# First stage reordered, normalization of later tiles on GpSimd, transposes set singly between matmuls

## The chip, the cores and the metric

The kernel runs on one core of a Trainium2 chip. The metric is the device time of one execution in microseconds, the median of several runs. The engines are TensorE (PE in the profile, with its weight loads as PEld), VectorE (DVE), ScalarE (ACT), GpSimd (POOL), and SyncE (SP), which here only issues DMAs.

## The reference

```python
xn = _layernorm(x, axis=-1)                       # x: 4 x 512 x 512, fp32
q = einsum('bpd,hde->bphe', xn, W_Q) + b_Q        # 16 heads of 128; k and v likewise
scores = where(causal, q k^T / sqrt(128), -100000)
s = einsum('bqhe,hed->bqd', softmax(scores) v, W_O) + b_O
g = silu(ffn(xn))                                 # gate, up (1408), silu, down, each with scales
out = x + s * g
```

## The kernel before

**Precision.** Every fp32 operand of a matmul is held as two fp32r parts: `hi`, a rounded copy made by ScalarE, and `lo`, the rest, made by a subtraction on VectorE or GpSimd. A product takes three matmuls. `mm3` (line 90) issues them for one chunk of the contraction: hi with lo, hi with hi, lo with hi. A projection has four chunks, so 12 matmuls.

**Order of the work.** All of it is written out by hand under a manual schedule: each engine runs its instructions in the order in which the program emits them, and waits in place for what an instruction needs. There are four batches of 512 tokens, each in four tiles `t` of 128, and 16 heads in groups of two. The attention loop (line 525) takes 64 steps `n`: group by group, within a group batch by batch, within a batch the two heads.

**One step of the loop.** `softmax` (272) issues the scores of head `n` (three banks), the row minima and sums (VectorE, ScalarE) and the scaling by GpSimd (line 316). `fill` then issues half of the work that the step has on the side: for the first head of a pair `project_v` (232) of two tiles. `turn_p` (319) transposes the probabilities through DRAM. Then come q and k of head `n+1` (`project`, 241), the product with v of head `n-1` (`attend`, 376), and the other half of `fill`.

**Normalization.** `ln_stats` (182, VectorE) and `ln_sd` (190, ScalarE) give mean and deviation of a tile; `ln_normalize` (208, VectorE: a reciprocal and one tensor_scalar) gives `xn`. `ln_transpose` (217) transposes a tile in four steps on TensorE into one PSUM bank, from pool `ps_st` for even tiles and `ps_mm` for odd ones; ScalarE copies the hi part, and `ln_low` (227, VectorE) makes the lo part. For batch `b+1` this happens in the first head of batch `b`, in group 0 only, so at n = 0, 2 and 4: the four `ln_normalize` stand between q and k (593), the four transposes and low parts after the rest of `fill` (606). Then the x tiles of batch `b+2` are loaded (610).

**PSUM.** Eight banks: three in `ps_st` (scores, transposes of even tiles), five in `ps_mm` (projections, v, products, transposes of odd tiles). A bank is taken again only when its last reader is done.

**First stage** (lines 461 to 514). SP loads the four x tiles of batch 0, then Wq, Wk of head 0 and Wv (two pieces). `warm_up` (202) keeps TensorE busy with 24 transposes meanwhile. Loaded weights wait in `pending`; `split_pending` (150) emits their hi copies (ScalarE) and lo parts (GpSimd). The first q and k are projected in two halves of 256 tokens (`parts=2`), both halves in one bank. `project` is a generator: a `next` issues one half's matmuls, and the following `next` its evacuation. The order is tiles 0 and 1, first half of q, tiles 2 and 3, first half of k, second halves of q and k, then `project_v` of tile 0.

Of the kernel before, what the change touches and what calls it, by code (L numbers as in the profile page):

```python
# [10 lines left out]
F32 = mybir.dt.float32  # L11
# [7 lines left out]
P = 128  # L19
# [1 line left out]
IGNORE = -100000.0  # L21
EPS = 1e-5
BIG = 3.0e38
WARM = 24
LOW_BITS = (1 << 12) - 1


# [15 lines left out]
def kernel(  # L43
# [46 lines left out]
    def mm3(ps, a, b, first, last):  # L90
        nc.tensor.matmul(ps, a.hi, b.lo, start=first, stop=False)  # L91
        nc.tensor.matmul(ps, a.hi, b.hi, start=False, stop=False)  # L92
        nc.tensor.matmul(ps, a.lo, b.hi, start=False, stop=last)  # L93


    with ExitStack() as at:
        lnp = at.enter_context(tc.tile_pool(name="lnp", bufs=NT))
# [14 lines left out]
        def load_x(b, t):  # L112
            xt = lnp.tile([P, D], F32, name="xt", tag="xt")
            nc.sync.dma_start(out=xt, in_=x[b, ts(t, P), :])
            x_in[b, t] = xt
# [14 lines left out]
            load_on[0].dma_start(out=r, in_=src)  # L130
            return r

        def split_w(dst, raw):
            nc.scalar.copy(dst.hi, raw)
            nc.gpsimd.tensor_tensor(dst.lo, raw, dst.hi32, ALU.subtract)

        def flat(s):
            return Split(s.hi.rearrange("p c e -> p (c e)"), s.lo.rearrange("p c e -> p (c e)"))
# [8 lines left out]

        pending = []

        def split_pending(n):  # L150

            for due, dst, raw in [p for p in pending if p[0] <= n]:
                split_w(dst, raw)
            pending[:] = [p for p in pending if p[0] > n]

        def prepare(due, dst, src, name):
# [3 lines left out]
        def prepare_qk(h, due, due_k=None):  # L160
            for d, src, n, when in ((wq, w_q, "wq", due), (wk, w_k, "wk", due_k or due)):
                d[h] = weight(wqkp, [P, ND, E], f"{n}{h}", n)
                prepare(when, flat(d[h]), src[h].rearrange("p c e -> p (c e)"), f"{n}r{h}")

        def prepare_v(g, due):
            wv[g] = weight(wvop, [P, ND, HG * E], f"wv{g}", "wv")
            half = ND // 2
            for i in range(2):
                c = slice(i * half, (i + 1) * half)
                src = w_v[g][:, c, :].rearrange("p c e -> p (c e)")  # L170
                prepare(due, flat(wv[g][:, c, :]), src, f"wvr{g}_{i}")
# [10 lines left out]
        def ln_stats(b, tt):  # L182

            mv = small.tile([P, len(tt), 2], F32, name="mv")
            for k, t in enumerate(tt):
                st = small.tile([P, 6], F32, name="st")
                nc.vector.bn_stats(out=st, in_=x_in[b, t])
                nc.vector.bn_aggr(out=mv[:, k, :], in_=st)
            mv_of[b, tuple(tt)] = mv

        def ln_sd(b, tt):
            mv = mv_of.pop((b, tuple(tt)))
            sd = small.tile([P, len(tt)], F32, name="sd")
            nc.scalar.activation(sd, mv[:, :, 1], AF.Sqrt, bias=eps)
            for k, t in enumerate(tt):
                ln_of[b, t] = mv[:, k, :], sd[:, k : k + 1]

        def table(func):

            nc.scalar.activation(small.tile([P, 1], F32, name="junk"), eps, func)  # L200
# [4 lines left out]
            for k in range(WARM):  # L205
                nc.tensor.transpose(junk[:, k % NT, :], ident, ident)

        def ln_normalize(b, t):
            xt = x_in.pop((b, t))
            mv, sd = ln_of.pop((b, t))  # L210
            rstd = small.tile([P, 1], F32, name="rstd")
            nc.vector.reciprocal(rstd, sd)
            xn = lnp.tile([P, D], F32, name="xn")
            nc.vector.tensor_scalar(xn, xt, mv[:, 0:1], rstd, ALU.subtract, ALU.mult)
            xn_of[b, t] = xn

        def ln_transpose(b, t):
            xn = xn_of.pop((b, t))
            pool, tag = ((ps_st, "st"), (ps_mm, "mm"))[t % 2]
            tr = pool.tile([P, ND, P], F32, name="tr", tag=tag)  # L220
            for c in range(ND):
                nc.tensor.transpose(tr[:, c, :], xn[:, ts(c, P)], ident)
            to = xnT[b][:, :, ts(t, P)]
            nc.scalar.copy(to.hi, tr)
            lo_of[b, t] = lambda: nc.vector.tensor_tensor(to.lo, tr, to.hi32, ALU.subtract)  # L225

        def ln_low(b, t):
            lo_of.pop((b, t))()
# [2 lines left out]

        def project_v(g, b, t):
            ps = ps_mm.tile([P, HG * E], F32, name="psv", tag="mm")
            for c in range(ND):
                mm3(ps, xnT[b][:, c, ts(t, P)], wv[g][:, c, :], c == 0, c == ND - 1)
            v = weight(vp, [P, HG * E], f"v{g}_{b}_{t}", "v")
            nc.scalar.copy(v.hi, ps)
            nc.vector.tensor_tensor(v.lo, ps, v.hi32, ALU.subtract)
            v_of.setdefault((g, b), []).append(v)

        def project(b, h, w, bias, name, parts=1):

            ps = ps_mm.tile([P, S], F32, name="ps" + name, tag="mm")
            both = qkp.tile([P, 2, S], F32R, name=name, tag=name)
            q = Split(both[:, 0, :], both[:, 1, :])
            q.both = both
            for k in range(parts):
                at_ = ts(k, S // parts)
                for c in range(ND):
                    mm3(ps[:, at_], w[:, c, :], xnT[b][:, c, at_], c == 0, c == ND - 1)  # L250
                yield
                nc.scalar.activation(  # L252
                    q.hi[:, at_], ps[:, at_], AF.Identity, bias=bias[:, h : h + 1]
                )
                nc.vector.scalar_tensor_tensor(  # L255
                    q.lo[:, at_], ps[:, at_], bias[:, h : h + 1], q.hi32[:, at_],
                    ALU.add, ALU.subtract,
                )
            yield q

# [199 lines left out]

        with tc.manual_schedule():
            nc.gpsimd.memset(eps, EPS)
            for t in range(NT):
                load_x(0, t)
            prepare_qk(0, -4, -3)
            prepare_v(0, -2)
            bq_sb, bk_sb, bv_sb, gs_sb, us_sb = small_const()
            table(AF.Sqrt)
# [4 lines left out]
            nc.gpsimd.memset(ones, 1.0)  # L473
            nc.gpsimd.memset(mask, 0.0)
            make_causal_mask(nc, mask[:, S - P :], mask_val=IGNORE / SCALE)
            ln_stats(0, [0])
            ln_sd(0, [0])
            ln_stats(0, [1])
            ln_sd(0, [1])
            ln_normalize(0, 0)  # L480
            split_pending(-4)
            ln_transpose(0, 0)
            ln_stats(0, [2])
            ln_sd(0, [2])
            ln_normalize(0, 1)
            ln_low(0, 0)
            split_pending(-3)
            ln_transpose(0, 1)
            ln_low(0, 1)
            q_of = project(0, 0, wq[0], bq_sb, "q", 2)  # L490
            k_of = project(0, 0, wk[0], bk_sb, "k", 2)
            next(q_of)
            split_pending(-2)
            prepare_qk(1, -1)
            ln_stats(0, [3])
            ln_sd(0, [3])
            ln_normalize(0, 2)
            ln_transpose(0, 2)
            ln_normalize(0, 3)
            ln_low(0, 2)  # L500
            ln_transpose(0, 3)
            next(k_of)
            ln_low(0, 3)
            next(q_of)
            next(k_of)
            split_pending(-1)
            table(AF.Exp)
            qT = next(q_of)
            kT = next(k_of)
            for t in range(NT):  # L510
                load_x(1, t)
            bo_bc = load_const(b_o.broadcast_to([P, D]), [P, D], "bo_bc")
            ds_bc = load_const(down_s.broadcast_to([P, D]), [P, D], "ds_bc")
            project_v(0, 0, 0)

            load_on[0] = nc.scalar
            heads = [(g, b, i) for g in range(NG) for b in range(B) for i in range(HG)]
# [7 lines left out]
            for n, (g, b, i) in enumerate(heads):  # L525
# [12 lines left out]
                def fill(ks):  # L538
                    for t in ks:
                        if i == 0 and not (n == 0 and t == 0):  # L540
                            project_v(g, b, t)
                        if i == HG - 1 and prev is not None:
                            project_out(*prev, t, zs[prev])
# [40 lines left out]
                if nxt is not None:  # L584
                    if ln_b is not None and n != 1:
                        ln_stats(ln_b, range(NT))
                    nh = nxt[0] * HG + nxt[2]
                    *_, qT = project(nxt[1], nh, wq[nh], bq_sb, "q")
                    if n == 0:
                        ln_sd(ln_b, range(NT))  # L590
                        table(AF.Exp)
                    if ln_next:
                        for t in range(NT):
                            ln_normalize(b + 1, t)
                if nxt is not None:
                    *_, kT = project(nxt[1], nh, wk[nh], bk_sb, "k")
                    raw = raw_next
# [4 lines left out]
                if ln_b is not None and n > 0:  # L602
                    ln_sd(ln_b, range(NT))
                    table(AF.Exp)
                if ln_next:
                    fill(range(half, NT))
                    for t in range(NT):
                        ln_transpose(b + 1, t)
                        ln_low(b + 1, t)
                    if b + 2 < B:  # L610
                        for t in range(NT):
                            load_x(b + 2, t)
# [191 lines left out]
```

## Time and profile before

| | us |
|---|---|
| median of 3 runs | 1222.99 (1222.97 to 1223.63) |
| profiled execution, time | 1222.41 |
| profiled execution, span of the trace | 1220.6 |
| PE / PEld busy | 1206.5 / 1052.7 |
| DVE / ACT / POOL busy | 827.1 / 525.3 / 301.7 |
| first scores of head 0 start | 20.58 |
| first attention step's end (scores of head 1 start) | 34.20 |
| feed-forward part starts | 974.0 |

A row of the timeline has the start and the duration in us, the engine, the line in the code, the instruction with its output and inputs, how many rows were merged (x4), and in brackets the idle time before it with what ended it. A row of the waits names the waiting instruction, what it waited for, the sum in us, the number of times and the longest. A row of the clock by stretches gives for each stretch the busy time and count of each engine, the clock that TensorE was granted (1.00 is full), the share of DMA and its rate.

### The profile page before, as it was taken

How to read it: one execution, taken by the hardware profiler on the slowest of the kernel's cores; microseconds unless marked ns; L12 is line 12 of the kernel's file. 1: busy time of each engine (PE TensorE's matmuls, PEld its weight loads, DVE VectorE, ACT ScalarE, POOL GpSimd, SP SyncE). 2: the span in 40 equal slices, each digit the busy share in tenths (PEclk: the TensorE clock that was granted, in tenths of full speed). 3: DMA queues.
4: the chain of work that ended last, by engine and by line, in shares of the span. 5: the costliest groups of instructions: out<-in, count | busy, mean ns of one | idle time of the engine just before them, and what ended most of it. 6: DMA issues, size and time to landing. Idle time of an engine off the chain costs nothing.

```text
span 1220.6 us, 18887 instructions
## 1 busy us (share of the span) xinstructions
PE 1206.5 (99%) x6514; PEld 1052.7 (86%) x6514; DVE 827.1 (68%) x2044; ACT 525.3 (43%) x1169; POOL 301.7 (25%) x433
## 2 busy tenths in 40 slices
PE   8999999999999999999999999999999999999997
PEld 8888888888888888888888888888888888888886
DVE  6897777777777777777877676767677533434343
ACT  5654444444445445444544454445444342323231
POOL 4212321232123213321412141214121341212010
PEclk9999999999999999999999999999999999999999
DMA  4454456656665667566655565555544893627241
GB/s 161 138 175 147 145 165 206 206 179 190 190 207 174 203 198 218 181 208 192 211 182 173 178 189 175 177 185 173 173 156 156 272 317 93 207 87 213 80 147 38
DMA packets 117912, 215.55 MB, mean 177 GB/s; under 512 B 13232, under 2 KB 45744, under 8 KB 117808
## 3 DMA queue, kind: packets, MB, share of 16 engines
q1 hardware_dynamic: 74016, 134.51, 34.4%
q10 hardware_dynamic: 29376, 53.26, 14.2%
q0 software_dynamic: 14416, 26.48, 7.9%
q8 instruction: 53, 0.87, 0.3%
q14 instruction: 51, 0.42, 0.1%
HBM read 135.17 MB, written 79.04 MB: 175 GB/s over the span
## 4 chain that ended last, share of the span: by engine, by line
PE 95%; DVE 3%; ACT 1%; DMA 0%; issue 0%; SPq 0%; DVEq 0%; ACTq 0%
PE z L387 10%; PE pd L667 7%; PE pg L667 7%; PE pu L667 7%; PE pso L91 5%; PE psv L91 5%; PE pso L92 5%; PE pso L93 5%; PE psv L93 5%; PE psv L92 5%; PE psq L91 5%; PE psq L92 5%; PE psq L93 5%; PE psk L91 5%; PE psk L92 5%; PE psk L93 5%
## 5 line engine op out<-in xcount | busy, mean ns | idle before, releaser
L316 POOL TENSOR_SCALAR p<-p,rtot 128x512 f32<-128x512 f32 (+3 forms) x256 | 148.2, 598 | 675.1 <-DVE rtot L315 675.1
L312 ACT ACTIVATE p<-p,nmax 128x512 f32<-128x512 f32 (+3 forms) x256 | 140.9, 552 | 147.3 <-DVE nmax L298 147.3
L358 DVE TENSOR_TENSOR ptl<-ptr,pth 128x640 fp32r<-128x640 f32 x126 | 133.7, 1099 | 1.4 <-ACT pth L357 1.4
L330 DVE STREAM_TRANSPOSE sq<-p 128x256 f32<-128x256 f32 x378 | 113.3, 361 | 0.0
L298 DVE CUSTOM_DVE_ANT_0 p<-sc,mask 128x512 f32<-128x512 f32 (+2 forms) x192 | 96.5, 552 | 0.3 <-PE sc L93 0.3
L252 ACT ACTIVATE k<-psk,consts 128x512 fp32r<-128x512 f32 (+1 forms) x65 | 44.2, 681 | 108.7 <-PE psk L93 108.6
L252 ACT ACTIVATE q<-psq,consts 128x512 fp32r<-128x512 f32 (+1 forms) x65 | 44.3, 682 | 97.2 <-PE psq L93 72.6
L357 ACT CAST pth<-ptr 128x640 fp32r<-128x640 f32 x126 | 84.9, 724 | 0.1
L413 DVE TENSOR_TENSOR a<-pso,a 128x512 f32<-128x512 f32 x108 | 72.1, 686 | 17.7 <-PE pso L93 16.4
L255 DVE SCALAR_TENSOR_TENSOR k<-psk,consts,k 128x512 fp32r<-128x512 f32 (+1 forms) x65 | 48.0, 739 | 52.8 <-ACT k L252 52.7
L693 DVE SCALAR_TENSOR_TENSOR hd<-pu,consts,sg 128x512 f32<-128x512 f32 x44 | 33.0, 751 | 66.8 <-PE pu L667 62.2
L315 DVE RECIPROCAL rtot<-tot 128x1 f32<-128x1 f32 x256 | 41.6, 162 | 42.7 <-ACT p L312 36.3
L91 PE MATMUL sc<-k,q 128*128 128x512 f32 (+2 forms) x192 | 65.7, 342 | 1.7 <-DVE xl L225 1.7
L93 PE MATMUL sc<-k,q 128*128 128x512 f32 (+2 forms) x192 | 64.7, 337 | 0.0
L92 PE MATMUL sc<-k,q 128*128 128x512 f32 (+2 forms) x192 | 64.7, 337 | 0.0
L255 DVE SCALAR_TENSOR_TENSOR q<-psq,consts,q 128x512 fp32r<-128x512 f32 (+1 forms) x65 | 47.6, 732 | 7.6 <-ACT q L252 7.6
L312 ACT ACTIVATION_READ_ACCUMULATOR p<-p,nmax 128x1 f32 x256 | 47.8, 187 | 0.0
L91 PEld LDWEIGHTS sc<-k,q 128*128 128x128 f32 x192 | 36.2, 188 | 7.9 <-DVE xl L225 3.5
L723 ACT ACTIVATE o<-o 128x512 f32<-128x512 f32 (+1 forms) x17 | 10.3, 607 | 68.8 <-DVE o L722 68.8
L92 PEld LDWEIGHTS sc<-k,q 128*128 128x128 f32 x192 | 36.2, 189 | 3.6
L93 PEld LDWEIGHTS sc<-k,q 128*128 128x128 f32 x192 | 36.1, 188 | 2.6
L691 ACT ACTIVATE sg<-pg,consts 128x512 f32<-128x512 f32 x44 | 30.3, 688 | 17.0 <-PE pg L667 17.0
(734 smaller groups left out, 3811.6 us busy)
## 6 DMA issues: line engine op xcount, KB each, us to landing
turn<-sq SPq DMA_DIRECT2D x63, 640.0 KB, 3.8
ptr<-turn SPq DMA_DIRECT2D x252, 160.0 KB, 3.4
acc<-a SPq DMA_DIRECT2D x124, 256.0 KB, 3.7
a<-acc ACTq DMA_DIRECT2D x108, 256.0 KB, 2.8
xt<-in_x SPq DMA_DIRECT2D x16, 256.0 KB, 4.1
wor<-in_w_o ACTq DMA_DIRECT2D x16, 256.0 KB, 4.5
fa<-acc SPq DMA_DIRECT2D x16, 256.0 KB, 5.9
fx<-in_x SPq DMA_DIRECT2D x16, 256.0 KB, 6.9
```

The source lines that it names most:

```text
L91: nc.tensor.matmul(ps, a.hi, b.lo, start=first, stop=False)
L92: nc.tensor.matmul(ps, a.hi, b.hi, start=False, stop=False)
L93: nc.tensor.matmul(ps, a.lo, b.hi, start=False, stop=last)
L252: nc.scalar.activation(q.hi[:, at_], ps[:, at_], AF.Identity, bias=bias[:, h : h + 1])
L255: nc.vector.scalar_tensor_tensor(q.lo[:, at_], ps[:, at_], bias[:, h : h + 1], q.hi32[:, at_], ALU.add, ALU.subtract,)
L298: nc.vector.tensor_tensor_reduce(out=of[t], in0=where[t], in1=add, scale=-SCALE, scalar=BIG, op0=ALU.add, op1=ALU.min, accum_out=nmax[t],)
L312: nc.scalar.activation(of[t], of[t], AF.Exp, bias=nmax[t], scale=-1.0, accum_out=tot)
L316: nc.gpsimd.tensor_scalar(of[t], of[t], rtot, 1.0, ALU.mult, ALU.mult)
L330: nc.vector.transpose(dst.rearrange("p a s i -> p s a i"), src.rearrange("p (s a i) -> p s a i", s=n, i=Q),)
L358: nc.vector.tensor_tensor(dst(pt.lo), src, dst(pt.hi32), ALU.subtract)
L387: nc.tensor.matmul(o, v, p_, start=k == 0, stop=k == len(todo) - 1)
L667: nc.tensor.matmul(ps, l, r, start=first and k == 0, stop=last and k == len(pairs) - 1)
```

## The change

The loads, splits, normalizations and projections of the first stage change their order. The tiles 2 and 3 of batch 0, and all tiles of the later batches, are normalized on GpSimd; the reciprocals stay on VectorE. The low parts of Wv of group 0 are made on VectorE. `warm_up` has 20 transposes. `mm3_all` takes the place of `mm3` in the projections of q, k and v: first hi with hi for all four chunks, then the products with the first operand's lo part, then those with the second's; in `project` the second operand is x. After each of its matmuls it takes one entry from `side`, if there is any. At n = 0, 2 and 4 `side` holds, for each tile of the next batch, its four transposes and then its low part (20 entries), so that they stand one by one between the 24 matmuls of `project_v` for tiles 2 and 3. The halves of q and k get a tile of `ps_mm` each. In the first stage v of tile 0 moves ahead of the second halves, the table load for Exp ahead of the casts of Wv, and the split of head 1's weights behind the last evacuation.

```diff
@@ -21,7 +21,7 @@
 IGNORE = -100000.0
 EPS = 1e-5
 BIG = 3.0e38
-WARM = 24
+WARM = 20
 LOW_BITS = (1 << 12) - 1
 
 
@@ -92,6 +92,21 @@
         nc.tensor.matmul(ps, a.hi, b.hi, start=False, stop=False)
         nc.tensor.matmul(ps, a.lo, b.hi, start=False, stop=last)
 
+    def mm3_all(ps, pairs):
+        todo = [
+            (getattr(a, i), getattr(b, k))
+            for i, k in (("hi", "hi"), ("lo", "hi"), ("hi", "lo"))
+            for a, b in pairs
+        ]
+        for n, (l, r) in enumerate(todo):
+            nc.tensor.matmul(ps, l, r, start=n == 0, stop=n == len(todo) - 1)
+            if side:
+                side.pop(0)()
+    side = []
 
     with ExitStack() as at:
         lnp = at.enter_context(tc.tile_pool(name="lnp", bufs=NT))
@@ -130,9 +145,9 @@
             load_on[0].dma_start(out=r, in_=src)
             return r
 
-        def split_w(dst, raw):
+        def split_w(dst, raw, on=nc.gpsimd):
             nc.scalar.copy(dst.hi, raw)
-            nc.gpsimd.tensor_tensor(dst.lo, raw, dst.hi32, ALU.subtract)
+            on.tensor_tensor(dst.lo, raw, dst.hi32, ALU.subtract)
 
         def flat(s):
             return Split(s.hi.rearrange("p c e -> p (c e)"), s.lo.rearrange("p c e -> p (c e)"))
@@ -147,10 +162,10 @@
 
         pending = []
 
-        def split_pending(n):
+        def split_pending(n, on=nc.gpsimd):
 
             for due, dst, raw in [p for p in pending if p[0] <= n]:
-                split_w(dst, raw)
+                split_w(dst, raw, on)
             pending[:] = [p for p in pending if p[0] > n]
 
         def prepare(due, dst, src, name):
@@ -205,24 +220,37 @@
             for k in range(WARM):
                 nc.tensor.transpose(junk[:, k % NT, :], ident, ident)
 
-        def ln_normalize(b, t):
+        def ln_normalize(b, t, on=nc.vector):
             xt = x_in.pop((b, t))
             mv, sd = ln_of.pop((b, t))
             rstd = small.tile([P, 1], F32, name="rstd")
             nc.vector.reciprocal(rstd, sd)
             xn = lnp.tile([P, D], F32, name="xn")
-            nc.vector.tensor_scalar(xn, xt, mv[:, 0:1], rstd, ALU.subtract, ALU.mult)
+            on.tensor_scalar(xn, xt, mv[:, 0:1], rstd, ALU.subtract, ALU.mult)
             xn_of[b, t] = xn
 
         def ln_transpose(b, t):
+            for step in ln_transposes(b, t):
+                step()
+        def ln_transposes(b, t):
             xn = xn_of.pop((b, t))
             pool, tag = ((ps_st, "st"), (ps_mm, "mm"))[t % 2]
-            tr = pool.tile([P, ND, P], F32, name="tr", tag=tag)
-            for c in range(ND):
-                nc.tensor.transpose(tr[:, c, :], xn[:, ts(c, P)], ident)
             to = xnT[b][:, :, ts(t, P)]
-            nc.scalar.copy(to.hi, tr)
-            lo_of[b, t] = lambda: nc.vector.tensor_tensor(to.lo, tr, to.hi32, ALU.subtract)
+            tr = []
+            def step(c):
+                if c == 0:
+                    tr.append(pool.tile([P, ND, P], F32, name="tr", tag=tag))
+                nc.tensor.transpose(tr[0][:, c, :], xn[:, ts(c, P)], ident)
+                if c == ND - 1:
+                    nc.scalar.copy(to.hi, tr[0])
+                    lo_of[b, t] = lambda: nc.vector.tensor_tensor(
+                        to.lo, tr[0], to.hi32, ALU.subtract
+                    )
+            return [lambda c=c: step(c) for c in range(ND)]
 
         def ln_low(b, t):
             lo_of.pop((b, t))()
@@ -231,8 +259,7 @@
 
         def project_v(g, b, t):
             ps = ps_mm.tile([P, HG * E], F32, name="psv", tag="mm")
-            for c in range(ND):
-                mm3(ps, xnT[b][:, c, ts(t, P)], wv[g][:, c, :], c == 0, c == ND - 1)
+            mm3_all(ps, [(xnT[b][:, c, ts(t, P)], wv[g][:, c, :]) for c in range(ND)])
             v = weight(vp, [P, HG * E], f"v{g}_{b}_{t}", "v")
             nc.scalar.copy(v.hi, ps)
             nc.vector.tensor_tensor(v.lo, ps, v.hi32, ALU.subtract)
@@ -240,21 +267,17 @@
 
         def project(b, h, w, bias, name, parts=1):
 
-            ps = ps_mm.tile([P, S], F32, name="ps" + name, tag="mm")
             both = qkp.tile([P, 2, S], F32R, name=name, tag=name)
             q = Split(both[:, 0, :], both[:, 1, :])
             q.both = both
             for k in range(parts):
                 at_ = ts(k, S // parts)
-                for c in range(ND):
-                    mm3(ps[:, at_], w[:, c, :], xnT[b][:, c, at_], c == 0, c == ND - 1)
+                ps = ps_mm.tile([P, S // parts], F32, name="ps" + name, tag="mm")
+                mm3_all(ps, [(w[:, c, :], xnT[b][:, c, at_]) for c in range(ND)])
                 yield
-                nc.scalar.activation(
-                    q.hi[:, at_], ps[:, at_], AF.Identity, bias=bias[:, h : h + 1]
-                )
+                nc.scalar.activation(q.hi[:, at_], ps, AF.Identity, bias=bias[:, h : h + 1])
                 nc.vector.scalar_tensor_tensor(
-                    q.lo[:, at_], ps[:, at_], bias[:, h : h + 1], q.hi32[:, at_],
-                    ALU.add, ALU.subtract,
+                    q.lo[:, at_], ps, bias[:, h : h + 1], q.hi32[:, at_], ALU.add, ALU.subtract
                 )
             yield q
 
@@ -460,9 +483,11 @@
 
         with tc.manual_schedule():
             nc.gpsimd.memset(eps, EPS)
-            for t in range(NT):
-                load_x(0, t)
+            load_x(0, 0)
+            load_x(0, 1)
             prepare_qk(0, -4, -3)
+            load_x(0, 2)
+            load_x(0, 3)
             prepare_v(0, -2)
             bq_sb, bk_sb, bv_sb, gs_sb, us_sb = small_const()
             table(AF.Sqrt)
@@ -473,45 +498,44 @@
             nc.gpsimd.memset(ones, 1.0)
             nc.gpsimd.memset(mask, 0.0)
             make_causal_mask(nc, mask[:, S - P :], mask_val=IGNORE / SCALE)
-            ln_stats(0, [0])
-            ln_sd(0, [0])
-            ln_stats(0, [1])
-            ln_sd(0, [1])
+            for t in range(2):
+                ln_stats(0, [t])
+                ln_sd(0, [t])
             ln_normalize(0, 0)
+            ln_normalize(0, 1)
+            ln_stats(0, [2])
             split_pending(-4)
             ln_transpose(0, 0)
-            ln_stats(0, [2])
+            ln_transpose(0, 1)
+            ln_low(0, 0)
+            ln_low(0, 1)
             ln_sd(0, [2])
-            ln_normalize(0, 1)
-            ln_low(0, 0)
             split_pending(-3)
-            ln_transpose(0, 1)
-            ln_low(0, 1)
+            ln_stats(0, [3])
+            ln_sd(0, [3])
+            table(AF.Exp)
+            ln_normalize(0, 2, nc.gpsimd)
+            ln_normalize(0, 3, nc.gpsimd)
+            split_pending(-2, nc.vector)
+            prepare_qk(1, -1)
             q_of = project(0, 0, wq[0], bq_sb, "q", 2)
             k_of = project(0, 0, wk[0], bk_sb, "k", 2)
             next(q_of)
-            split_pending(-2)
-            prepare_qk(1, -1)
-            ln_stats(0, [3])
-            ln_sd(0, [3])
-            ln_normalize(0, 2)
+            next(k_of)
             ln_transpose(0, 2)
-            ln_normalize(0, 3)
+            ln_transpose(0, 3)
             ln_low(0, 2)
-            ln_transpose(0, 3)
-            next(k_of)
             ln_low(0, 3)
+            project_v(0, 0, 0)
             next(q_of)
             next(k_of)
-            split_pending(-1)
-            table(AF.Exp)
             qT = next(q_of)
             kT = next(k_of)
+            split_pending(-1)
             for t in range(NT):
                 load_x(1, t)
             bo_bc = load_const(b_o.broadcast_to([P, D]), [P, D], "bo_bc")
             ds_bc = load_const(down_s.broadcast_to([P, D]), [P, D], "ds_bc")
-            project_v(0, 0, 0)
 
             load_on[0] = nc.scalar
             heads = [(g, b, i) for g in range(NG) for b in range(B) for i in range(HG)]
@@ -591,7 +615,7 @@
                         table(AF.Exp)
                     if ln_next:
                         for t in range(NT):
-                            ln_normalize(b + 1, t)
+                            ln_normalize(b + 1, t, nc.gpsimd)
                 if nxt is not None:
                     *_, kT = project(nxt[1], nh, wk[nh], bk_sb, "k")
                     raw = raw_next
@@ -603,10 +627,12 @@
                     ln_sd(ln_b, range(NT))
                     table(AF.Exp)
                 if ln_next:
+                    for t in range(NT):
+                        side.extend(ln_transposes(b + 1, t))
+                        side.append(lambda t=t: ln_low(b + 1, t))
                     fill(range(half, NT))
-                    for t in range(NT):
-                        ln_transpose(b + 1, t)
-                        ln_low(b + 1, t)
+                    while side:
+                        side.pop(0)()
                     if b + 2 < B:
                         for t in range(NT):
                             load_x(b + 2, t)
```

## The prediction

> **What bounds it now.** I read the page first: busy times, then the waits of TensorE, then the timeline of the first 100 us engine by engine, then the clock by stretches.
>
> ```profile
> PE 1206.5 (99%) x6514; PEld 1052.7 (86%) x6514; DVE 827.1 (68%) x2044; ACT 525.3 (43%) x1169; POOL 301.7 (25%) x433
> ```
>
> TensorE is busy for all but 14 us of 1220.6, and the chain that ended last is 95% TensorE. So only its idle time and its clock can be won, and the waits tell where they lie:
>
> ```profile
> PE psq L91 <- DVE xl L225: 2.1, 1, 2.1
> PE sc L91 <- DVE xl L225: 1.7, 4, 0.6
> ...
> PE tr L222 <- DVE k L255: 0.7, 1, 0.7
> PE psq L91 <- DVE q L255: 0.4, 1, 0.4
> ```
>
> The first and last row belong to the first stage (before 20.58 us), the others to the changes of batch. I number these T1, T2, T3 (heads 0, 2, 4). In the clock by stretches (the column before the last two is the granted clock), the first wait costs more than itself:
>
> ```profile
> 8.00:10.00 2.00, 0.10 (x1) 0.00 (x0) 1.19 (x2) 2.00 (x6) 2.00 (x2) 1.00 0.08 28
> 10.00:12.00 2.00, 1.75 (x9) 1.76 (x10) 1.90 (x6) 0.80 (x2) 2.00 (x3) 0.64 0.64 176
> 12.00:14.00 2.00, 2.00 (x12) 2.00 (x11) 1.31 (x1) 0.18 (x1) 1.03 (x1) 0.51 0.92 330
> ```
>
> TensorE idles from 8.1 to 10.25 us, and then has half its clock from 10.56 to 13.99: 256-column matmuls start 0.21 us apart there, 0.12 later.
>
> **Two rules of the Trainium skill.** "TensorE: Matmul & The Clock Gate", Part 1, says that the clock is halved after an idle window of 3413 ns, and that the windows run freely. The rows above agree: 3.43 us at half clock after a window with 2.15 us of idle. A window need not be wholly idle, then. At T2 about 1.25 us of idle (62.25, 64.17 and 65.36 us below) fell into 3.4 us and the clock stayed at 1.00. I put the threshold between 1.25 and 2.15 us per window, from this trace. "GPSIMD Engine Reference", 1. Specifications, says that GpSimd shares its SBUF interfaces with VectorE, which meets VectorE instructions in a two-port mode or with two SBUF inputs. The trace agrees: VectorE's normalization takes 0.55 us alone and 1.31 beside GpSimd's subtraction (10.34 to 13.04 us).
>
> ```profile
> 12.01 1.31 DVE L214 TENSOR_SCALAR xn<-xt,mv,rstd 128x512 f32<-128x512 f32 x1
> ...
> 58.85 0.14 DVE L212 RECIPROCAL rstd<-sd 128x1 f32<-128x1 f32 x1
> 59.02 0.55 DVE L214 TENSOR_SCALAR xn<-xt,mv,rstd 128x512 f32<-128x512 f32 x1
> ```
>
> **First stage, loads.** SP issues one load per 0.45 us. Wq moves from place 5 to 3, Wk from 6 to 4, x tiles 2, 3 from 3, 4 to 5, 6. By place the loads landed at 3.6, under 4.4, about 4.8, 5.5, 7.15, 7.8 us. So Wq is there at 4.8 instead of 7.15, x tile 2 only at 7.15.
>
> **First stage, up to the first projection.** Four warm-up transposes less (0.22 each) free TensorE at 5.9 instead of 6.8. VectorE has tile 0 normalized at 5.95 and, with no statistics of tile 2 between, tile 1 at 6.55 (before 7.4). ScalarE casts Wq (0.62) behind tile 1's deviation, by 6.3; GpSimd's low part takes 1.27, to 7.6. Transposes of tiles 0, 1 run 6.1 to 7.7; their casts (0.58 each) end at 8.4. The new order of a projection uses x's low part last, so q starts at 8.45 (before 10.25) and its 12 matmuls end at 9.9: statistics of tile 2 hold VectorE to 7.95, the two low parts (0.68 each) end at 9.25, in time. The idle is 0.7 us, so I expect no half clock.
>
> **First stage, the rest.** k waits for Wk's low part: cast after tile 2's deviation, 8.6 to 9.25, GpSimd 9.3 to 10.6; k ends 11.6. Behind it GpSimd normalizes tile 2 by 11.3 and tile 3 by 12.0 (0.69 each, the row of L316 below); their transposes (0.11 each) end 12.5. ScalarE has its deviation of tile 3 at 10.4, now the table load (1.28 + 0.2), to 11.8, only then the two casts of Wv (to 12.95) and those of tiles 2, 3 (to 14.05). So v runs 12.5 to 14.2, waiting about 0.4, VectorE taking 0.68 for each low part of Wv. q's second half starts 14.2, ends 15.65 (low part of tile 3 at 15.1). k's second half is the sixth tile in five banks: it needs the bank of q's first half, whose low part VectorE finishes at 15.95. The own banks remove the 0.5 us wait of 15.65 to 16.17, and leave 0.3. k ends 17.4. Before, v stood behind it and covered its evacuation; now nothing does: 0.5 on ScalarE, 0.5 on VectorE. The first scores start at **18.6 instead of 20.58: 2.0 us gained**, with ends of 1.0 (half clock after all) and 2.8.
>
> **GpSimd's norm at T1 to T3.** No row shows it; the nearest is the same operation and shape with other scalars:
>
> ```profile
> 23.83 0.69 POOL L316 TENSOR_SCALAR p<-p,rtot 128x512 f32<-128x512 f32 x1 [3.19 <-DVE rtot L315]
> ```
>
> I take 0.69; bounds 0.55 (as VectorE) and 1.3 (its two-input row). It takes four norms, 2.2 us, off VectorE, which is a gain only where TensorE waits for VectorE.
>
> **Transposes between matmuls.** In a run they start 0.109 apart (16 from 93.82 to 95.56). Singly no row shows them. The nearest is a 128-column matmul between wide ones (43.04 us): the z group of 1280 columns takes 0.63 where 512, 384 and 256 alone take 0.23, 0.17 and 0.12, so it costs 0.11. I take 0.11, no difference; bounds 0.06 and 0.16, or 0.8 us either way for each T.
>
> **Where they wait.** Now the first transpose stands behind the first matmul of v tile 2, 23 matmuls (2.7 us) sooner than before, and TensorE's queue is in order: the rest of v and the next head's scores are queued behind it. At T1, from the first scores on: v tile 2 starts after 8.7 us as before; VectorE ends q's low part at 10.2 (statistics of four tiles ahead of it, 3.2 us; x lands long before), reciprocal, GpSimd, tile 0 ready at 11.1. TensorE stalls 2.2. Then 16 x 0.11 + 23 x 0.12 = 4.5 and the scores 1.76: 17.4. Before, this was 16.71, with the score waits. **T1 loses 0.7.** GpSimd is also later with head 0's probabilities, since the low parts of head 1's weights (2.6) and two DMA issues (1.3) now stand ahead of them; VectorE's own work hides all but 0.15 of it.
>
> ```profile
> 57.10 0.28 PE L91 MATMUL psv<-wv0l,xh 128*128 128x256 f32 x1
> ...
> 62.25 0.66 PE L222 MATMUL tr<-ident,xn 128*128 128x128 f32 x4 [0.66 <-DVE k L255]
> ...
> 64.17 0.44 PE L91 MATMUL sc<-k,q 128*128 128x384 f32 x1 [0.56 <-DVE xl L225]
> ...
> 65.36 0.39 PE L91 MATMUL sc<-k,q 128*128 128x256 f32 x1 [0.41 <-DVE xl L225]
> ```
>
> T2 before takes 8.9 us from 57.10 to the next group at 65.99. The waits shown go (k's low part no longer stands behind four norms; the low parts come before the scores need their banks), but tile 0 is ready only 1.75 (reciprocal at 58.85) + 0.95 = 2.7 after the start: stall 2.6, then 4.5 + 1.76, sum 9.0. **T2 loses 0.1.** At T3 VectorE has q's low part 2.6 us ahead of v tile 2, nothing stalls, and the 0.3 to 0.4 us of score waits go: **T3 gains 0.3.** The next x loads on SP wait for the norms on GpSimd instead of VectorE; they are wanted 12 us later, so nothing. Matmul order within a projection: nothing, the gate and down products pair operands differently and both start 0.226 apart.
>
> **Sum.** 2.0 - 0.7 - 0.1 + 0.3 = 1.5 us off the profiled execution's 1222.41 (span 1220.6 and 1.8 around it). That execution lies 0.58 under the median of 1222.99, so the median would be **1221.5**, -0.12%. About 0.2% (2.4 us) is what a measurement can tell from no change.
>
> **Rivals.** (a) *The new stalls halve the clock.* Each of T1, T2 idles 2.2 to 2.6 us, as much as the 2.15 that did it in the first stage. If one window holds over 1.25 to 2.15 of it, the next 3.4 us run at half, 1.7 us lost. For it: the size. Against: the windows run freely, and a stall split over two may pass. Once: 1223.2. (b) *Both times*: 1221.5 + 3.4 = 1224.9, slower than before; it decides from two stalls over the threshold in one window each. (c) *GpSimd gets tile 0 sooner or the first stage gains its upper end*, VectorE relieved at T1: 1.0 to 2.0 more, 1219.8. (d) *A single transpose costs its upper bound*: +2.4, 1223.9. (e) The new scores' wait eats the first stage: gain 1.0 there, 1222.5.
>
> **Chances.** Forecast 0.37, (a) 0.23, (b) 0.10, (c) 0.20, (d) 0.05, (e) 0.05. Range 1218.8 to 1224.3: (c) and its spread below, most of (a), (d) and part of (b) above. Faster by over 0.2% (under 1220.5): most of (c) and a fifth of the forecast, 0.27. Slower (over 1225.4): part of (b), some of (d), 0.08. The rest, 0.65, within.
>
> **What would show it.** q's first matmul near 8.5 us with a clock of 1.00 until 18 us; a wait of scores for k L255 of about 1 us near 18; waits of transposes for POOL of 2.2 and 2.6 us at T1 and T2, and no wait of scores for xl L225. Right or wrong of (a) is the clock in the 3.4 us after those. Wrong would be: no stall on POOL, or single transposes further apart than 0.24 us.

## The result and the profile after

The changed kernel takes 1236.03 us (median; 1234.54 to 1239.66) where the kernel before takes 1222.98 on the same chip: a ratio of 1.011, 95% interval 1.0095 to 1.0126. It is 13 us slower; the forecast was 1221.5. The profiled execution took 1237.78, its span 1236.0, 15.4 more than before.

The busy times, then the waits of TensorE (who waited for whom: us in total, times, longest):

```profile
PE 1209.8 (98%) x6510; PEld 1055.2 (85%) x6510; DVE 820.6 (66%) x2032; ACT 526.6 (43%) x1169; POOL 330.3 (27%) x445
```

```profile
PE tr L246 <- POOL xn L229: 14.6, 9, 4.1
...
PE sc L91 <- DVE k L279: 1.1, 1, 1.1
...
PE psq L103 <- ACT xh L248: 0.7, 1, 0.7
```

The waits for xl and q of before are gone, as forecast, and so is most of q's first wait (0.7 for 2.1). In their place stand 14.6 us of transposes waiting for GpSimd. GpSimd is 28.6 us busier, with 14 normalizations more and the two low parts of Wv less. The rows of the normalization's line, for GpSimd and for VectorE (duration min/median/max in ns) say why:

```profile
L229 POOL TENSOR_SCALAR xn<-xt,mv,rstd x14: 2068/2074/3025, 10.0 to 107.8; 128x512 f32<-128x512 f32 x14
L229 DVE TENSOR_SCALAR xn<-xt,mv,rstd x2: 545/546/548, 5.4 to 6.1; 128x512 f32<-128x512 f32 x2
```

One takes 2.07 us on GpSimd, not 0.69, the time of the row that I took for it, and lies outside the bound of 1.3. At T1 TensorE stands behind the first v matmul (start, duration, idle time in brackets):

```profile
31.51 0.28 PE L103 MATMUL psv<-wv0h,xh 128*128 128x256 f32 x1
35.45 0.40 PE L246 MATMUL tr<-ident,xn 128*128 128x128 f32 x1 [3.66 <-POOL xn L229]
35.53 0.52 PE L103 MATMUL psv<-wv0h,xh 128*128 128x256 f32 x1
35.86 0.41 PE L246 MATMUL tr<-ident,xn 128*128 128x128 f32 x1
```

The transposes then come 0.42 us apart, since the stall was paid a second time, in the clock (the clock by stretches, granted clock third from the right):

```profile
14.00:16.00 2.00, 0.83 (x5) 0.83 (x5) 0.14 (x1) 0.00 (x0) 1.12 (x1) 0.78 0.18 67
16.00:18.00 2.00, 2.00 (x11) 2.00 (x10) 0.69 (x1) 0.59 (x1) 0.00 (x0) 0.50 0.49 131
...
36.00:38.00 2.00, 2.00 (x11) 1.75 (x10) 0.22 (x1) 0.59 (x1) 2.00 (x2) 0.50 0.65 145
...
70.00:72.00 2.00, 1.39 (x8) 1.12 (x6) 0.69 (x1) 0.47 (x1) 2.00 (x2) 0.50 0.92 234
```

Read from the starts of TensorE's groups, the 15.4 us lie at the four places that the forecast named, and nowhere else. From the end of T1 to v tile 2 of T2 it is 19.81 us before and 19.65 after, from T2 to T3 24.95 and 24.96, from T3 to the end 1122.95 and 1122.9.

| us | before | forecast | after |
|---|---|---|---|
| first scores of head 0 start | 20.58 | 18.6 | 22.70 |
| T1, from there to q of head 2 | 16.71 | 17.4 | 22.13 |
| T2, from v tile 2 to the next group but the scores | 8.89 | 9.0 | 14.43 |
| T3, likewise | 6.71 | 6.4 | 9.22 |

### The profile page after: what moved, and what is told of

It reads as the page before. It is cut to its first block, busy times and chain, and to the rows that moved or that the text cites. A ratio compares the mean times of both kernels' runs of the same rounds, so it can differ in the third digit from the quotient of the medians.

```text
span 1236.0 us, 18895 instructions
## 1 busy us (share of the span) xinstructions
PE 1209.8 (98%) x6510; PEld 1055.2 (85%) x6510; DVE 820.6 (66%) x2032; ACT 526.6 (43%) x1169; POOL 330.3 (27%) x445
## 4 chain that ended last, share of the span: by engine, by line
PE 94%; DVE 2%; POOL 2%; issue 1%; ACT 1%; DMA 1%; SPq 0%; POOLq 0%; DVEq 0%; ACTq 0%
PE psv L103 14%; PE psq L103 13%; PE psk L103 13%; PE z L410 10%; PE pd L693 6%; PE pg L693 6%; PE pu L693 6%; PE pso L91 5%; PE pso L93 5%; PE pso L92 5%; PE sc L91 3%; PE sc L93 3%; PE sc L92 3%; POOL xn L229 1%; PE sc L312 1%
## 5 line engine op out<-in xcount | busy, mean ns | idle before, releaser
L338 DVE RECIPROCAL rtot<-tot 128x1 f32<-128x1 f32 x256 | 41.7, 163 | 42.6 <-ACT p L335 36.3
```

## The experiments

Theory A was that the 2.07 us of GpSimd's normalization are the whole loss, and that the rest of the forecast stands. Theory B was that the loss comes from the places of the transposes, the new order of matmuls or the order of the first stage. Each ratio below is to the kernel before on the same chip. The parts (first scores, T1 to T3) are read from one profiled execution of each kernel.

**Normalization back on VectorE** (all else of the change stays)

```diff
-            ln_normalize(0, 2, nc.gpsimd)
-            ln_normalize(0, 3, nc.gpsimd)
+            ln_normalize(0, 2)
+            ln_normalize(0, 3)
...
-                            ln_normalize(b + 1, t, nc.gpsimd)
+                            ln_normalize(b + 1, t)
```

> The changed kernel with all normalizations on VectorE; everything else of the change stays. Theory A (the loss is GpSimd's normalization, 2.07 us a tile instead of the 0.69 assumed, which TensorE waits for): about 1221 to 1224.5, that is the forecast's sum (first stage -2, T1 -0.7, T2 -0.1, T3 +0.3) plus 1.7 for each half-clock window. Theory B (the loss is in the places of the transposes, the order of matmuls or the order of the first stage): still above 1231.

Measured: 1222.22, ratio 0.9999 (0.9991 to 1.0008). The 13 us are gone; theory B is out as their cause. The parts of its profiled execution: first scores at 18.18, T1 18.98, T2 9.01, T3 6.39, against a forecast of 18.6, 17.4, 9.0, 6.4. T1 is 1.6 above it and has one window at half clock (below, at the filling).

**A cheap form on GpSimd**

```diff
-            on.tensor_scalar(xn, xt, mv[:, 0:1], rstd, ALU.subtract, ALU.mult)
+            if on is nc.gpsimd:
+                on.tensor_scalar(xn, xt, rstd, 1.0, ALU.mult, ALU.mult)
+            else:
+                on.tensor_scalar(xn, xt, mv[:, 0:1], rstd, ALU.subtract, ALU.mult)
```

> The changed kernel with GpSimd's tensor_scalar as x times rstd times 1.0, the form of the probabilities' scaling (0.69 us); the subtraction of the mean is left out. Theory A: an instruction of 0.69 us and the time that was forecast, 1221.5, or up to 1225 with half-clock windows. Theory B: above 1231 as the changed kernel. If GpSimd's time depends on place or neighbours and not on the form, the instruction stays near 2.07 us and so does the time.

Measured: 1224.15, ratio 1.0013 (1.0006 to 1.0019). GpSimd's four normalizations of T1:

```profile
28.99 2.69 POOL L230 TENSOR_SCALAR xn<-xt,rstd 128x512 f32<-128x512 f32 x4 [4.74 <-DVE rstd L227]
```

They take 2.69 us together, 0.67 each, in the same places of the program: it is the form that costs. The parts are 18.38, 19.25, 10.85 and 6.39, and the clock is at half from 30.9 to 34.3 and from 61.6 to 65.0 us. This is rival (b), two half-clock windows: it was put at 1224.9.

**Which form is slow.** Ten forms, in batches 1 to 3 (operands in the order of the operations)

```diff
+                (1, 1): (m, 1.0, ALU.subtract, ALU.mult),
+                (1, 2): (rstd, 1.0, ALU.mult, ALU.mult),
+                (1, 3): (rstd, 0.5, ALU.mult, ALU.add),
+                (2, 0): (rstd, rstd, ALU.mult, ALU.mult),
+                (2, 1): (rstd, m, ALU.mult, ALU.add),
+                (2, 2): (2.0, 0.5, ALU.mult, ALU.mult),
+                (2, 3): (m, rstd, ALU.add, ALU.mult),
+                (3, 0): (m, m, ALU.subtract, ALU.subtract),
+                (3, 1): (1.0, rstd, ALU.mult, ALU.mult),
+                (3, 2): (0.5, rstd, ALU.subtract, ALU.mult),
```

> The changed kernel with other operations in GpSimd's tensor_scalar, tile by tile (only these ten tiles' normalization is changed, so batches 1 to 3 are not normalized rightly). What makes it 2.07 us: two operands from pointers (then mult, mult with rstd twice takes 2.07 and subtract with a pointer, mult with 1.0 takes 0.69), or the pair of operations (then mult, mult is 0.69 with any operands, and subtract, mult 2.07 even with 1.0), or the subtraction alone. Theory A expects some forms at 0.69 and some at 2.07; if all but one are at 2.07, mult, mult is a special case.

Measured, GpSimd's timeline at T2 (2, 0 to 2, 3) and T3 (3, 0 to 3, 3, the last with the change's own form):

```profile
65.92 0.77 POOL L243 TENSOR_SCALAR xn<-xt,rstd 128x512 f32<-128x512 f32 x1 [0.64 <-DVE rstd L227]
66.67 0.77 POOL L243 TENSOR_SCALAR xn<-xt,rstd,mv 128x512 f32<-128x512 f32 x1
67.41 0.62 POOL L243 TENSOR_SCALAR xn<-xt 128x512 f32<-128x512 f32 x1
68.02 0.77 POOL L243 TENSOR_SCALAR xn<-xt,mv,rstd 128x512 f32<-128x512 f32 x1
...
92.81 2.08 POOL L243 TENSOR_SCALAR xn<-xt,mv 128x512 f32<-128x512 f32 x1
97.38 2.69 POOL L243 TENSOR_SCALAR xn<-xt,rstd 128x512 f32<-128x512 f32 x2 [2.49 <-DVE rstd L227]
100.05 2.08 POOL L243 TENSOR_SCALAR xn<-xt,mv,rstd 128x512 f32<-128x512 f32 x1
```

Two pointers instead of one cost 0.08, so they are not it; and at T1 subtract with one pointer, then mult with 1.0, still took 2.00. Add then mult of the same operands takes 0.77, subtract then mult 2.08. The row at 97.38 holds one quick and one slow form: mult, mult with 1.0 and rstd, then 2.01 for subtract with a constant. The next kernel asks whether it is subtract alone.

**More forms, and the two-tensor subtraction.** Other pairs at T1 and T2 (1, 2 and 2, 3, not shown, repeat add, mult), and add or mult in ten low parts of weights

```diff
+                (1, 0): (rstd, m, ALU.mult, ALU.subtract),
+                (1, 1): (2.0, 0.5, ALU.subtract, ALU.mult),
+                (1, 3): (m, rstd, ALU.max, ALU.mult),
+                (2, 0): (m, rstd, ALU.add, ALU.add),
+                (2, 1): (rstd, m, ALU.mult, ALU.max),
+                (2, 2): (m, rstd, ALU.min, ALU.mult),
```

> Other operations in GpSimd's instructions in the changed kernel (the normalization of batches 1 and 2 is not right, and ten low parts of weights are sums or products instead of differences, so the outputs are not the reference's). If subtract is slow in either place of tensor_scalar: mult, subtract about 2.0 us and subtract with two immediates 2.0, add, mult and add, add 0.77. max and min show whether add and mult alone are quick. If subtract of two tensors is slow too, the low parts by add take less than 1.29 us.

Measured on GpSimd's timeline, which has the first two at T1, the first two at T2, and then one low part by add (wq2l) and one by mult (wk3l):

```profile
31.96 2.08 POOL L244 TENSOR_SCALAR xn<-xt,rstd,mv 128x512 f32<-128x512 f32 x1 [4.69 <-issue]
34.01 1.93 POOL L244 TENSOR_SCALAR xn<-xt 128x512 f32<-128x512 f32 x1
...
63.87 2.08 POOL L244 TENSOR_SCALAR xn<-xt,mv,rstd 128x512 f32<-128x512 f32 x1 [0.63 <-DVE rstd L230]
65.94 2.06 POOL L244 TENSOR_SCALAR xn<-xt,rstd,mv 128x512 f32<-128x512 f32 x1
...
129.16 1.29 POOL L152 TENSOR_TENSOR wq2l<-wqr,wq2h 128x512 fp32r<-128x512 f32 x1 [1.94 <-ACT wq2h L149]
...
147.81 1.29 POOL L152 TENSOR_TENSOR wk3l<-wkr,wk3h 128x512 fp32r<-128x512 f32 x1
```

The row at 63.87 is add, add: 2.08, where I expected 0.77. So it is not subtract that is slow. Of the pairs tried, three are quick (mult, mult; mult, add; add, mult) and the others, with subtract, max, min or two adds, take 1.93 to 2.08 (subtract and max in either place, min in the first alone). Why these three pairs are quick no run shows. The low parts of weights take 1.29 us with add and with mult, and 1.28 to 1.30 with subtract; some of each operation took up to 1.9. So between two tensors the operation makes no difference.

**The mean added negated**

```diff
+            nm = small.tile([P, len(tt)], F32, name="nm")
+            nc.vector.tensor_scalar(nm, mv[:, :, 0], -1.0, 1.0, ALU.mult, ALU.mult)
...
-            on.tensor_scalar(xn, xt, mv[:, 0:1], rstd, ALU.subtract, ALU.mult)
+            on.tensor_scalar(xn, xt, nm_of[b, t], rstd, ALU.add, ALU.mult)
```

> The changed kernel with GpSimd adding the negated mean instead of subtracting the mean (VectorE negates the means once for each set of statistics). Theory A with its cause, that subtract is what is slow: 0.77 us a tile as in the run of forms, and the time of the cheap form and a little more, 1224 to 1225, against 1236 of the changed kernel. If the cheap time came from one pointer operand or from leaving the mean out, it stays at 2.07 us and 1236.

Measured: 1225.86, ratio 1.0022 (1.0013 to 1.0031), four normalizations in 3.0 us:

```profile
32.35 3.01 POOL L233 TENSOR_SCALAR xn<-xt,nm,rstd 128x512 f32<-128x512 f32 x4 [4.98 <-DVE rstd L231]
```

The form is confirmed with the full computation; the time is 1 us above the expectation, and that is a chain of its own. With the negation in `ln_stats` tile 0's normalization starts at 5.99 us instead of 5.40 (0.2 of it from a later load). Then VectorE's normalization of tile 1 met GpSimd's low part of Wq (VectorE's timeline):

```profile
6.64 1.52 DVE L233 TENSOR_SCALAR xn<-xt,nm,rstd 128x512 f32<-128x512 f32 x1
```

That is 1.52 instead of 0.55, TensorE waited 2.3 us for tiles 0 and 1, two windows ran at half clock (7.9 to 14.7; a third came at T2), and the first scores started at 21.50 instead of 18.2.

**GpSimd alone, on the kernel before**

```diff
-                            ln_normalize(b + 1, t)
+                            ln_normalize(b + 1, t, nc.gpsimd)
```

> The kernel before with only the normalizations of batches 1 to 3 on GpSimd; transposes stay in a run behind v. Theory A: the last of four tiles is ready 8.3 us after the first reciprocal, so T1 loses about 4.4, T2 3.7, T3 1.5, together 9.6: about 1232.6, plus half-clock windows. Theory B: 1223, no loss, since neither places nor orders change.

Measured: 1235.75, ratio 1.0114 (1.0099 to 1.013). Nothing else of the change is in it, and it loses as much as the whole change: T1 22.81, T2 14.51, T3 8.26. Beside the 3 us above the expectation stand four windows at half clock, from 36.3 to 43.1 and 70.5 to 77.3 us.

**Transposes in a run again**, with VectorE's normalization

```diff
-                        side.extend(ln_transposes(b + 1, t))
-                        side.append(lambda t=t: ln_low(b + 1, t))
-                    fill(range(half, NT))
-                    while side:
-                        side.pop(0)()
+                    fill(range(half, NT))
+                    for t in range(NT):
+                        ln_transpose(b + 1, t)
+                        ln_low(b + 1, t)
```

> The changed kernel with all normalizations on VectorE and the transposes of batches 1 to 3 in a run behind v, as before: what remains is the new first stage and the new order of matmuls. If the places of the transposes cost what was forecast (T1 -0.7, T2 -0.1, T3 +0.3, and the half clock behind their stalls 1.7): the first stage's 2.4 us remain, 1220.0, with no half clock after 14 us. If the places cost nothing: 1222.2 as with VectorE and single transposes.

Measured: 1220.45, ratio 0.9981 (0.9974 to 0.9988). First scores at 18.32, T1 16.83, T2 8.94, T3 6.70, no half clock at all. This is in the main the new first stage's gain, since T1 to T3 are within 0.12 us of before. So the single places cost about 2 us (0.9981 against 0.9999) with the normalization on VectorE.

**The same with the negated mean on GpSimd**, at first with the negation in `ln_stats`, then beside the reciprocals of GpSimd's tiles alone:

> The changed kernel with GpSimd adding the negated mean and the transposes in a run behind v. If single places are what loses and VectorE's relief is a gain where the transposes stand late enough: T1 gains about 1.0, T2 1.7, T3 0.3 beside the first stage's 2.4, so about 1217. If VectorE's relief is worth nothing: 1220, as with VectorE.

Measured: 1221.31, ratio 0.9986 (0.998 to 0.9993); the profiled execution lost the first stage in the chain just told (first scores at 21.59), while T1 (16.15) and T2 (7.43) gained.

```diff
+            if on is nc.gpsimd:
+                nm = small.tile([P, 1], F32, name="nm")
+                nc.vector.tensor_scalar(nm, mv[:, 0:1], -1.0, 1.0, ALU.mult, ALU.mult)
+                on.tensor_scalar(xn, xt, nm, rstd, ALU.add, ALU.mult)
```

> As the run with the negated mean and transposes in a run, but the means are negated beside the reciprocals of the tiles that GpSimd takes, so nothing is added ahead of tiles 0 and 1. If that earlier delay (0.4 us, a collision with GpSimd's subtraction that made tile 1's normalization 1.52 us, and the half clock behind it) was what cost it the first stage's gain: scores of head 0 start near 18.3 instead of 21.6 and the time is about 1218.8. If the add form itself costs elsewhere: 1221 to 1222 as before.

Measured: **1218.94, ratio 0.9969 (0.9958 to 0.998)**, better than both kernels. First scores at 18.21, T1 16.11, T2 7.46, T3 6.71; 0.6 of it is given back at n = 4, whose scores wait for VectorE's low part of k. Its waits, among which no transpose waits for a normalization any more:

```profile
PE sc L91 <- DVE k L284: 1.4, 2, 1.1
...
PE psq L103 <- ACT xh L253: 0.7, 1, 0.7
PE z L415 <- DVE ptl L386: 0.2, 1, 0.2
```

**The stall filled**, with VectorE's normalization and single transposes

```diff
+                    if b < 2:
+                        side.append(lambda: warm_up(16))
                     for t in range(NT):
                         side.extend(ln_transposes(b + 1, t))
```

> The changed kernel with all normalizations on VectorE, single transposes, and 16 idle transposes of the identity (1.7 us) in front of the first single transpose at T1 and T2, in the time in which TensorE waits anyway. If the stall of 2.1 to 2.4 us costs a window of half clock because TensorE does nothing in it: the window at 30.5 to 34 goes and the time is about 1220.5, 1.7 less than without the filling. If not: 1222.2.

Measured: 1220.30, ratio 0.9981 (0.9974 to 0.9989), against 0.9999 without the filling. The clock by stretches, first of the kernel without it, then with it:

```profile
28.00:30.00 2.00, 0.73 (x6) 0.73 (x7) 1.89 (x7) 1.97 (x4) 0.00 (x0) 1.00 0.56 159
30.00:32.00 2.00, 2.00 (x14) 2.00 (x12) 1.96 (x5) 0.92 (x3) 0.00 (x0) 0.62 1.07 196
32.00:34.00 2.00, 2.00 (x11) 2.00 (x11) 1.50 (x3) 1.04 (x3) 0.00 (x0) 0.53 1.01 331
```

```profile
28.00:30.00 2.00, 1.86 (x18) 1.66 (x16) 1.89 (x7) 1.61 (x3) 0.00 (x0) 1.00 0.40 107
30.00:32.00 2.00, 2.00 (x20) 2.00 (x19) 1.93 (x6) 1.55 (x4) 0.00 (x0) 1.00 1.01 225
32.00:34.00 2.00, 2.00 (x19) 2.00 (x19) 2.00 (x5) 1.37 (x4) 0.00 (x0) 1.00 1.00 308
```

Work without use in the idle time gives about 2 us back: rival (a)'s mechanism, with its price of 1.7. With it the single places are as good as a run (0.9981 both), so what they cost was the half clock. The executions agree with that: without filling they spread from 1220.6 to 1224.2 us, and the mean granted clock falls into three groups, as with no, one and two such windows: 0.999 (three executions, 1220.6 to 1221.0), 0.997 to 0.998 (six, 1221.7 to 1222.4) and 0.995 (four, 1223.0 to 1224.2). With filling they take 1219.9 to 1221.7, in a run 1220.0 to 1220.9, all at 0.998 or 0.999.

**v of tile 0 behind k again**

```diff
-            project_v(0, 0, 0)
             next(q_of)
             next(k_of)
             qT = next(q_of)
             kT = next(k_of)
+            project_v(0, 0, 0)
```

> The new first stage with VectorE's normalization and transposes in a run (1220.4 on another chip), and v of tile 0 behind k's second half again. If v's place is what opens the 1.1 us wait of the first scores: the wait goes and the time is about 1219.3. If v in the earlier place covers as much waiting for the casts of tiles 2 and 3: a wait of about 1 us shows in front of q's second half instead, and the time is 1220.4.

Measured: 1221.42, ratio 0.9991 (0.9984 to 0.9997), not better than with v ahead (0.9981). The scores' wait is gone and stands in front of q's second half:

```profile
11.10 1.03 PE L246 MATMUL tr<-ident,xn 128*128 128x128 f32 x8
13.48 0.74 PE L103 MATMUL psq<-xh,wq0h 128*128 128x256 f32 x4 [1.35 <-ACT xh L248]
```

The first scores start at 17.98, a little earlier, but T1 takes 17.76 against 16.83, and transposes wait for the normalization there. That v's evacuation stands on VectorE ahead of the softmax again, and delays T1, is my reading; I did not try it apart.

## Why the prediction was wrong, and where it was right

**The step that failed** is "GpSimd's norm at T1 to T3": "the nearest is the same operation and shape with other scalars", 0.69 with an upper bound of 1.3. The row was of mult, mult; the change's is subtract, mult, and on GpSimd that takes 2.07. "Other scalars" hid the only thing that mattered, and no rival gave a chance even to the bound of 1.3. The Trainium skill, "GPSIMD Engine Reference", 3.1 Elementwise, gives 769 ns for 512 elements in the best case. The 0.77 measured for add, mult agrees; mult, mult with two constants took less (0.62), and subtract, mult at 2.07 is far from that case; the measurement decides. With 2.07 the same working would have put the last tile of T1 8.3 us behind its reciprocal instead of 2.8.

**Two terms follow from it.** In the first stage tiles 2 and 3 were put at 11.3 and 12.0 and came at 12.1 and 15.1; the second took 3.03, beside VectorE's low parts of Wv (two SBUF inputs, 12.0 to 13.3). GpSimd's two normalizations, and the transposes that waited for the second:

```profile
10.02 5.10 POOL L229 TENSOR_SCALAR xn<-xt,mv,rstd 128x512 f32<-128x512 f32 x2
...
15.17 1.11 PE L246 MATMUL tr<-ident,xn 128*128 128x128 f32 x4 [2.37 <-POOL xn L229]
```

With a window at half clock behind it, the first stage was 2.1 us longer than before, where 2.0 less was forecast. At T1, T2 and T3 the first tile is later by 1.4 and each further one too, and rival (a)'s half clock came at T1 and twice in a row at T2.

**Right, shown by the run with VectorE's normalization:** the first scores at 18.2 (forecast 18.6), T2 at 9.01 (9.0), T3 at 6.39 (6.4), T1 at 18.98, or 17.3 without the 1.7 of its half-clock window (17.4). The cheap form on GpSimd comes to the same: without a window each, T1 17.5, T2 9.1, and T3 6.39. With VectorE q's first matmul came at 8.08 (8.45) at full clock, single transposes and v matmuls 0.23 apart (0.23), the scores' wait for k 1.1 us (about 1), and the waits for xl went. The order of matmuls within a projection cost nothing: the stretches between T1, T2 and T3 are as long as before (19.65 for 19.81, 24.96 for 24.95).

**Undersized:** rivals (a) and (b). I gave the half clock 0.33 together and the forecast without it 0.37. With a cheap form both windows came (1224.15), with VectorE one in the profiled execution (1222.22 in the median). A stall of 2.2 to 2.6 us, as large as the one that did it in the trace of before, should have been the likelier case: of the 13 executions with VectorE's normalization ten lie in the groups with a window. Where a stall falls in the clock's own windows decides (last section), and that differs from one execution to the next. Rival (c) holds only with the transposes in a run: VectorE's relief is then worth 1.5 us at T2 (8.94 to 7.46) and 0.7 at T1 (16.83 to 16.11).

## What to carry to other kernels

A row of the trace stands for another instruction only if the operations are the same too; on GpSimd, take any other pair of operations as unmeasured, with a wide upper bound, and measure it alone first. Work that is spread between others is put where its input is ready, since an in-order queue turns an early place into a stall of everything behind it. Price a stall of TensorE of 2 us or more at its length and, unless it is known to fall across two windows of the clock, at another 1.7, and look whether idle work can hold the clock.

## What the runs showed of the hardware

- GpSimd's tensor_scalar on 128x512 fp32 takes 0.62 to 0.77 us for mult, mult, for mult, add and for add, mult, and 1.93 to 2.08 for every other pair tried: subtract in either place, max, min, and add, add. VectorE takes 0.55 for subtract, mult.
- GpSimd's operation between two tensors (128x512) took 1.26 to 1.30 at its quickest, with subtract, add and mult alike.
- Where the two engines ran side by side, the one that started later took longer. VectorE's normalization took 1.52 instead of 0.55 just behind the start of GpSimd's subtraction of two tensors (6.64 and 6.61 us, first run with the negated mean). In the fastest run it started ahead (6.10 and 6.29), took 0.55, and the subtraction 1.49 instead of 1.27. GpSimd's normalization took 3.03 instead of 2.07 behind VectorE's subtraction of two tensors (12.1 and 11.96, changed kernel).
- Transposes hold the clock as matmuls do: 16 of the identity in the stall of T1 kept it at 1.00, where it fell to 0.53 without them.
- The clock keeps windows of its own. Half clock began in the changed kernel at 15.1, 35.6 and 69.7 us, which lie 6 and 10 times 3.41 us apart. I counted TensorE's idle time along this grid, up to 1200 us, in the nine traces with a half-clock window there. All 17 windows of full clock with 1.95 us or more of idle were followed by one at half clock, and none with 1.86 or less. So the prediction's threshold, put between 1.25 and 2.15, lies between 1.86 and 1.95 here, and the idle need not be one stall: in the first run with the negated mean parts of two waits (1.30 and 0.97 us) were enough, 1.95 us together between 4.49 and 7.90. A longer stall that falls across two windows passes: 2.40 us at T2 with VectorE (1.70 in one window) and 2.58 at T1 with the negated mean (1.37) cost no clock. A window already at half clock was followed by another with 0.61 us or more of idle, and by full clock with 0.47 or less.
